# Split matmuls in attention and scan, and other rounds for front's halves, norms and weight sums: a change to a four-layer float32 kernel

## The chip, the cores and the metric

The kernel runs on one core of a Trainium2 chip. The metric is the device time of one execution in microseconds (us), as the median of several runs. A profile of one more execution shows each engine's instructions: PE (matrix products, with the weight loads as a row of their own), DVE (vector work), ACT (activation functions and copies), POOL (elementwise work beside DVE) and SP, which here only issues DMAs.

## The reference

The input x is 2 sequences of 2048 rows of 256 numbers, all float32. Four layers are added to it in turn, each on a layernorm of x:

```python
x = x + attn_a(layernorm(x))   # rmsnorm, q/kv/a = xn @ w_qkva; a linear scan along the rows, s = sigmoid(a)*s + kv; q*s
x = x + ffn(layernorm(x))      # gelu(x @ tern(W1).T + b1) @ tern(W2).T + b2, 256 -> 1024 -> 256
x = x + attn_b(layernorm(x))   # 16 heads of 64: per row, with states carried on,
                               #   G += k (k C)^T;  S += k k^T;  C += q v^T;  o = q (S C - G);  then o @ W_o
x = x + ffn(layernorm(x))      # the same weights again
```

`tern` rounds a weight matrix to -1, 0 and 1 by its own mean size.

## The kernel before

x stays on the chip as 32 chunks of 128 rows. The order of work on PE, DVE, ACT and POOL is written out by hand: each of these engines runs its instructions in the order in which the program issues them. PSUM has eight banks, which are dealt out in rings.

**Front** (`front`) does the scan layer and the first ffn. A block is four chunks (512 rows), and there are eight blocks, 0 to 7. After a start in which the first scans run, a loop makes one round per block: `ffn_in` gives eight tiles of the hidden layer (PE, then Gelu on ACT), `Hidden.split` cuts each pair of them into a rounded high half `hh` (ACT) and a rest `hl` (DVE), and `ffn_out` multiplies both by the second weight (64 matmuls) and adds the result to x. Both are generators, and `run(steps, n)` issues n pieces of one, so that other work stands between them. In rounds 0 to 3 the scan of a later block (`scan_steps`) is issued between pieces of `ffn_in`. Helpers prepare the rows of later blocks: `fs_` makes the layernorm statistics (DVE and POOL), `fq_` the normed rows (ACT), turned by a transposition in 32 x 32 squares on DVE and a way out to DRAM and back, and `fe_` the high and low halves of the turned rows (a cast on ACT, a subtraction on DVE) that `ffn_in` reads. `then` is a list of three steps that start attention's first chunk pair: its statistics, its rows, its turned rows. `later` holds the sums of attention's weights, `weights_kv`, four operations of 128 x 512 on POOL for each of wk, wv and wq.

**Attention** (`attention`) works through 32 steps: chunk n of sequence 0, then of sequence 1, for n = 0 to 15. Two steps of the same n are a pair. The products that make k, q and v of a pair (`Seven`) use a scheme with seven half-size products instead of eight, numbered 1 to 7, so they need sums of the weights (`weights_kv`) and of the turned rows (`pair_sums`, POOL). A kN or vN product is one matmul call with 512 columns, a qT product four calls with 128. One float32 matmul call is two matmul instructions, each with its weight load. The scan over rows is done in halves of 64 rows with 64 x 64 matmuls on quarters of PE's array, in bursts of 128 matmuls: `update` (hS, hM), `inter` with `products` (huT or hoT with hp), and `intra`. Between the bursts stand the products of `Seven` and the output products `outward` (hy).

**The last ffn** begins inside the last attention steps. The object `last` (class `Last`) prepares statistics, rows and halves there, and brings the rounded ffn weights back from DRAM: `weights` opens a generator of four DMAs of 256 KB, issued from ACT, and `part(n)` issues n of them; `part(None)` issues all that are left. Then a loop makes the remaining rounds. The very last block multiplies chunks 0 to 2 first and chunk 3 behind them; its result tile shares a bank with that of chunk 2.

Of the kernel before, what the change touches and what calls it, by code (L numbers as in the profile page):

```python
# [20 lines left out]
ALU = mybir.AluOpType  # L21
AX = mybir.AxisListType

P = 128
B, T, D = 2, 2048, 256
ND = D // P
# [18 lines left out]
def kernel(  # L45
# [333 lines left out]
        nc.vector.tensor_tensor(y, sc, pq, ALU.mult)  # L379
        return y  # L380

    def scan_steps(pool, g0, xnT, last, ys):

        def product(part, e):
            pq = bank([P, BT], f"pq{g0}_{e}_{part}")
            col = part * D + e * P
            for d in range(ND):
                nc.tensor.matmul(  # L388
                    pq, lhsT=wqkva[:, d, col : col + P], rhs=xnT[:, d, :], start=(d == 0), stop=(d == ND - 1),
                )  # L390
            return pq

        gate = [scan_gate(pool, g0, e) for e in range(ND)]
        for e in range(ND):
            nc.scalar.activation(gate[e], product(2, e), AF.Sigmoid)
        yield
        for e in range(ND):
            a, kq = gate[e], scan_pair(pool, g0, e)
            kv = product(1, e)
            sc = scan_line(pool, g0, e, BT, a, kq, kv, last)  # L400
            yield
            q = product(0, e)
            ys.append(kq[:, 1, :])
            nc.vector.tensor_tensor(kq[:, 1, :], sc, q, ALU.mult)
            yield
# [114 lines left out]
    def ffn_out(g0, hid, store=False, tag="ps"):  # L520

        banks = [bank([P, 2, D], f"o{g0}_{i}", tag) for i in range(2)]
        if store and g0 == blocks[-1]:
            order = [(f, range(BC - 1)) for f in range(NF)] + [(f, range(BC - 1, BC)) for f in range(NF)]
        else:
            order = [(f, range(BC)) for f in range(NF)]
        for f, cs in order:
            for c in cs:
                to = banks[c // 2][:, c % 2, :]
                for k, h in enumerate((hid.hi, hid.lo)):  # L530
                    nc.tensor.matmul(  # L531
                        to, lhsT=h[f // 2][:, f % 2, c * P : (c + 1) * P], rhs=w2r[:, f, :],
                        start=(f == 0 and k == 0 and c % 2 == 0), stop=(f == NF - 1 and k == 1),
                        skip_group_check=True,
                    )
                m = 1 if len(cs) < BC and c > 1 else 2
                if f == NF - 1 and (c % 2 == 1 or m == 1):
                    g = g0 + c + 1 - m
                    xs = x_sb[:, g : g + m, :]
                    nc.vector.tensor_tensor(xs, xs, banks[c // 2][:, c % 2 + 1 - m : c % 2 + 1, :], ALU.add)  # L540
                    if store:
                        nc.sync.dma_start(out=rows(of, g, m), in_=xs)
            yield
# [6 lines left out]
    def run(steps, n=None):  # L550
        for _ in steps if n is None else zip(range(n), steps):
            pass
# [4 lines left out]
    def front(scan_pool, ffn_pool, tern_pool, then, later):  # L557
# [21 lines left out]
        def fs_(i, between=None):  # L579
            fst[i] = norm_stats(ffn_pool, chunks(blocks[i]), bias=True, between=between)  # L580
# [89 lines left out]
        for i in range(NB):  # L670
            u, g0 = i + 5, blocks[i]
            more, scans = i + 1 < NB, u < len(units)
            hid, staged = hidden(ffn_pool, g0)
            steps = ffn_in(g0, fn.pop(i), hid, staged)
            if i == 0:
                ffn_bias(g0)
            if scans:
                ys[u] = []
                products = scan_steps(scan_pool, units[u][0], xnT[u], last[units[u][0] // CPB], ys[u])
                for j in range(4):  # L680
                    run(products, 1)
                    run(steps, 1)
                    if i == 0 and j == 0:
                        a_(4)
                        fq_(1)
                run(products)
                if i == 3:
                    fq_(5, scan_pool, "xn")
            else:
                run(steps, 4)  # L690
                if i == 4:
                    fs_(7)
                if i == NB - 2:
                    then[0]()
            if u + 1 < len(units):
                s_(u + 1)
            if i == 0:
                fs_(2)
            run(steps)
            if u + 1 < len(units):  # L700
                r_(u + 1)
            if i == 5:
                wq = const.tile([P, ND, H * DK], FP, tag="wq", name="wq")
                nc.sync.dma_start(out=wq, in_=w_q.rearrange("(c p) e -> p c e", p=P))
            if not more:
                wo = const.tile([P, NPR, D], FP, tag="wo", name="wo")
                nc.sync.dma_start(out=wo, in_=w_o.rearrange("(c p) e -> p c e", p=P))
                then[2]()

            steps = ffn_out(g0, hid, tag="out")  # L710
            if i > 3 and i - 4 < len(later):
                later[i - 4]()
            if i == 2:
                ffn_weights_away()
            if scans:
                fe_(i + 1)
                run(steps, 2)
                a_(u)
                run(steps, 3)
                if u + 1 < len(units):  # L720
                    t_(u + 1)
            if i < 3:
                fq_(i + 2)
                fs_(i + 3)
                if i == 2:
                    fs_(6)
            elif i == 3:
                fq_(6)
                fe_(5)
            elif i + 2 < NB:  # L730
                fe_(i + 2)
                if i + 3 < NB:
                    fq_(i + 3)
            if i == NB - 2:
                then[1]()
            run(steps)
            if more:
                ffn_bias(blocks[i + 1])

# [6 lines left out]
    def attention(keep, pool, state, last):  # L748
# [11 lines left out]
        def pair_sums(n):  # L760

            x = pairs[n]
            S = pool.tile([P, 4, P], FP, tag="S", bufs=1, name=f"S{n}")
            l, r = slice(0, P), slice(P, 2 * P)
            x11, x12, x21, x22 = x[:, 0, l], x[:, 1, l], x[:, 0, r], x[:, 1, r]
            for o, a, b_, op in (
                (S[:, 0, :], x21, x22, ALU.add), (S[:, 1, :], S[:, 0, :], x11, ALU.subtract),
                (S[:, 2, :], x11, x21, ALU.subtract), (S[:, 3, :], x12, S[:, 1, :], ALU.subtract),
            ):
                nc.gpsimd.tensor_tensor(o, a, b_, op)  # L770
            pairs[n] = x, S

        class Seven:

# [29 lines left out]
            def product(self, at, i, tag=None):  # L804

                new = tag is not None
                shape = [P, NPR // 2, P] if self.nm == "qT" else [P, HK]
                if new:
                    setattr(self, at, bank(shape, f"h{self.nm}{self.n}_{at}", tag))
                to = getattr(self, at)  # L810
                if self.nm == "qT":
                    for j in range(NPR // 2):
                        nc.tensor.matmul(  # L813
                            to[:, j, :], lhsT=self.B[i][:, j * P : (j + 1) * P], rhs=self.A[i],
                            start=(new and j == 0), stop=True, skip_group_check=True,
                        )
                else:
                    nc.tensor.matmul(  # L818
                        to, lhsT=self.A[i], rhs=self.B[i], start=new, stop=True, skip_group_check=True
                    )  # L820

            def add(self, c, at):
                nc.vector.tensor_tensor(self.C[c], self.C[c], getattr(self, at), ALU.add)  # L823
# [167 lines left out]

        NS = len(steps)
        pair_sums(0)
        stats = norm_stats(norm_pool, pair(1), bias=True)
        k, q, v = Seven(0, "kN", "oT"), Seven(0, "qT", "uT"), Seven(0, "vN", "oT")
        k.go(2, 1, 0, 5)
# [21 lines left out]
        for s in range(NS):  # L1018
# [24 lines left out]
                k.go(2)  # L1043
            if first and s > 0:
                units_end(s - 1)
            if s < NS - 1:
                last.part()
            if s >= 3:
                outward(s - 3, 1)
            intra(s, "S", "kN", "p1", "uT")  # L1050
# [119 lines left out]
            if s == NS - 3:  # L1170
                last.part(None)
                last.weights(False)
            if s >= 2:
                outward(s - 2, 0)
        last.out()
# [39 lines left out]
    class Last:  # L1215
# [10 lines left out]

        def stats(self, g0=None):
            g0 = self.g0 if g0 is None else g0
            self.st = [norm_stats(norm_pool, chunks(g0 + c, 2), bias=True) for c in (0, 2)]

        def rows(self, g0=None):
            g0 = self.g0 if g0 is None else g0
# [84 lines left out]
    with (  # L1317
# [7 lines left out]
        for _ in range(12):  # L1325
# [1 line left out]
        nc.scalar.activation(table, ones[:, :1], AF.Sigmoid)  # L1327
        front(
            scan_pool, ffn_pool, tern_pool, (attention_stats, attention_rows, attention_turned),
            [lambda: weights_kv(wk, wk_t), lambda: weights_kv(wv, wv_t), lambda: weights_kv(wq, wq_t)],  # L1330
        )
    front_ctx.close()

# [71 lines left out]
```

## Time and profile before

| | us |
|---|---|
| median of 3 runs | 1059.29 (1057.63 to 1059.35) |
| the profiled execution | 1060.83 |
| its span | 1059.0 |
| PE busy | 1044.0 |
| DVE busy | 730.8 |
| ACT busy | 613.4 |
| POOL busy | 201.7 |

Times inside the profile count from the start of the span. Front's rounds run from about 57 to 229 us, attention from there to about 945, the last rounds to the end. The chain that ended last lies on PE for 90% of the span. A row of a chain gives start, length, engine, tile and line; "issue" in it is time in which an engine waited for nothing that the profile shows. Ends of matmuls are modelled, so spacings from start to start are the better measure for them. A window's row gives its length, then busy time and number of instructions of PE, PE's weight loads, DVE, ACT and POOL, then the granted clock, the share of time the DMA engines were busy, and GB/s.

### The profile page before, as it was taken

The numbers are of one execution on the slowest core, as the hardware profiler recorded it, in microseconds if no ns is written. First come the engines' busy times: TensorE is split into PE (matmuls) and PEld (weight loads), VectorE is DVE, ScalarE is ACT, GpSimd is POOL, SyncE is SP. The second block draws the span as 40 slices with busy tenths as digits, with TensorE's granted clock in tenths as the row PEclk, the third lists the DMA queues.
The fourth block names the chain that finished last, engine by engine and source line by source line (L and its number), as shares of the span: only waits on it lengthen the run. The fifth ranks groups of instructions, "written<-read, shape, count | busy, mean of one in ns | idle before, by whom it ended". The sixth has DMA issues, their size and how long they took to land.

```text
span 1059.0 us, 43544 instructions
## 1 busy us (share of the span) xinstructions
PE 1044.0 (99%) x19920; PEld 805.4 (76%) x19920; DVE 730.8 (69%) x1047; ACT 613.4 (58%) x813; POOL 201.7 (19%) x314
## 2 busy tenths in 40 slices
PE   9999999999999999999999999999999999999998
PEld 7567778886777777777777777777777777889887
DVE  7987788856676765767666667666576666668873
ACT  4567778755645555455554555545545454658974
POOL 3433242831101001011010110100101020035540
PEclk9999999999999999999999999999999999999999
DMA  9231112203442423423324243243341334223321
GB/s 312 81 119 41 40 41 81 80 20 122 141 135 71 138 95 115 140 77 129 131 75 142 93 132 113 82 133 103 122 136 69 123 122 132 73 82 120 119 81 41
DMA packets 80825, 111.23 MB, mean 105 GB/s; under 512 B 8320, under 2 KB 66560, under 8 KB 80384
## 3 DMA queue, kind: packets, MB, share of 16 engines
q1 hardware_dynamic: 79024, 106.07, 30.2%
q8 instruction: 156, 2.56, 1.0%
q10 hardware_dynamic: 1584, 2.36, 0.9%
q14 instruction: 29, 0.24, 0.1%
q0 software_dynamic: 32, 0.00, 0.0%
HBM read 57.81 MB, written 50.59 MB: 102 GB/s over the span
## 4 chain that ended last, share of the span: by engine, by line
PE 90%; DVE 3%; ACT 2%; issue 2%; DMA 2%; POOL 1%; SPq 0%; ACTq 0%; DVEq 0%
PE hy L952 11%; PE o L531 9%; PE h L509 8%; PE hkN_X L818 6%; PE hqT_X L813 6%; PE hp L872 6%; PE hvN_X L818 6%; PE pq L368 4%; PE pq L388 3%; PE hS L929 3%; PE huT L889 3%; PE hoT L889 3%; PE huT L903 3%; PE hM L929 3%; PE hoT L903 3%; PE hqT_Z L813 3%
## 5 line engine op out<-in xcount | busy, mean ns | idle before, releaser
L878 DVE TENSOR_TENSOR p<-hp,mask 128x512 f32<-128x512 f32 x128 | 82.3, 683 | 83.4 <-PE hp L872 83.4
L952 PE MATMUL hy<-wo,oT 128*128 128x256 f32 x512 | 124.2, 386 | 0.0
L770 POOL TENSOR_TENSOR S<-xnT 128x128 f32<-128x128 f32 x30 | 13.8, 460 | 516.1 <-ACT xnT L312 516.1
L952 PEld LDWEIGHTS hy<-wo,oT 128*128 128x128 f32 x512 | 93.5, 190 | 20.6 <-issue 8.5
L494 DVE TENSOR_TENSOR hl<-h,hh 128x1024 fp32r<-128x1024 f32 x60 | 84.6, 1420 | 29.5 <-ACT hh L488 29.3
L515 ACT ACTIVATE h<-h,b_sb 128x512 f32<-128x512 f32 x120 | 77.9, 683 | 38.6 <-PE h L509 36.1
L914 ACT COPY uT<-huT 128x512 f32<-128x512 f32 x32 | 18.7, 586 | 124.9 <-PE huT L903 124.9
L194 ACT ACTIVATE xn<-x_sb,nb,rs 128x256 f32<-128x256 f32 x124 | 65.7, 594 | 21.9 <-POOL nb L180 20.1
L941 DVE TENSOR_TENSOR S<-S,hS 128x512 f32<-128x512 f32 x60 | 41.2, 687 | 43.2 <-PE hS L929 40.2
L259 DVE STREAM_TRANSPOSE squN<-uT 128x1024 f32<-128x1024 f32 x31 | 63.6, 2053 | 5.4 <-ACT uT L916 4.9
L971 ACT COPY uN<-rawuN 128x1024 f32<-128x1024 f32 x31 | 64.5, 2082 | 4.5 <-DMA rawuN<-dsquN 4.1
L259 DVE STREAM_TRANSPOSE sqkT<-kN 128x1024 f32<-128x1024 f32 x32 | 65.9, 2059 | 1.3 <-ACT kN L849 1.2
L971 ACT COPY kT<-rawkT 128x1024 f32<-128x1024 f32 x32 | 66.7, 2084 | 0.0
L488 ACT CAST hh<-h 128x1024 fp32r<-128x1024 f32 x60 | 63.1, 1051 | 1.9
L531 PE MATMUL o<-w2r,hl 128*128 128x256 f32 x256 | 61.3, 282 | 1.5 <-DVE hl L494 1.3
L531 PE MATMUL o<-w2r,hh 128*128 128x256 f32 x256 | 61.3, 281 | 0.0
L531 PE MATMUL o<-w2r_back,hh 128*128 128x256 f32 x248 | 60.4, 284 | 0.9 <-DVE x_sb L540 0.9
L531 PE MATMUL o<-w2r_back,hl 128*128 128x256 f32 x248 | 60.0, 281 | 0.0
L849 ACT COPY vN<-hvN_X 128x512 f32<-128x512 f32 x16 | 9.4, 587 | 78.8 <-PE hvN_X L818 78.8
L162 DVE BATCH_NORM_STATS2 st<-x_sb 128x6 f32<-128x256 f32 x128 | 51.2, 401 | 2.4 <-DMA x_sb<-in_x_dram 2.3
L823 DVE TENSOR_TENSOR kN<-kN,hkN_Y 128x512 f32<-128x512 f32 x16 | 11.0, 687 | 57.2 <-ACT kN L832 57.2
L531 PEld LDWEIGHTS o<-w2r,hl 128*128 128x128 f32 x256 | 48.2, 188 | 2.9 <-DVE hl L494 2.4
(227 smaller groups left out, 2554.3 us busy)
## 6 DMA issues: line engine op xcount, KB each, us to landing
dsqkT<-sqkT SPq DMA_DIRECT2D x32, 512.0 KB, 3.3
rawkT<-dsqkT SPq DMA_DIRECT2D x128, 128.0 KB, 3.0
dsquN<-squN SPq DMA_DIRECT2D x31, 512.0 KB, 3.3
rawuN<-dsquN SPq DMA_DIRECT2D x124, 128.0 KB, 3.1
dsqxn<-sqxn SPq DMA_DIRECT2D x14, 512.0 KB, 2.7
rawxn<-dsqxn SPq DMA_DIRECT2D x56, 128.0 KB, 2.9
out_dram<-x_sb SPq DMA_DIRECT2D x15, 256.0 KB, 2.9
x_sb<-in_x_dram SPq DMA_DIRECT2D x7, 512.0 KB, 8.9
```

The source lines that it names most:

```text
L194: nc.scalar.activation(xn[:, c, :], x_sb[:, g, :], AF.Identity, bias=nb[:, c : c + 1], scale=rs[:, c : c + 1],)
L259: nc.vector.transpose(to, src)
L494: nc.vector.tensor_tensor(self.lo[a], h, self.hi[a], ALU.subtract)
L509: nc.tensor.matmul(ph, lhsT=w1r[:, d, f * P : (f + 1) * P], rhs=r[:, d, :], start=(d == 0 and k == 0), stop=(d == ND - 1 and k == 1),)
L515: nc.scalar.activation(h[:, f % 2, :], ph, AF.Gelu, bias=b1_sb[:, f : f + 1])
L531: nc.tensor.matmul(to, lhsT=h[f // 2][:, f % 2, c * P : (c + 1) * P], rhs=w2r[:, f, :], start=(f == 0 and k == 0 and c % 2 == 0), stop=(f ...
L813: nc.tensor.matmul(to[:, j, :], lhsT=self.B[i][:, j * P : (j + 1) * P], rhs=self.A[i], start=(new and j == 0), stop=True, skip_group_check ...
L818: nc.tensor.matmul(to, lhsT=self.A[i], rhs=self.B[i], start=new, stop=True, skip_group_check=True)
L872: nc.tensor.matmul(banks[h][halves[c], p, :], lhsT=d[s][left][halves[h], p, halves[c]], rhs=d[s]["qT"][halves[h], p, halves[c]], start=Tru ...
L878: nc.vector.tensor_tensor(d[s][nm][:, h], banks[h], mask8, ALU.mult)
L952: nc.tensor.matmul(py, lhsT=d[s]["oT"][:, p, :], rhs=wo[:, p, :], start=(p == 0), stop=(p == NPR - 1),)
L971: act(t, d[s]["r" + nm].rearrange("p t q -> p q t"))
```

## The change

Five parts. Matmul calls of 512 columns are split into two of 256 columns: in `scan_steps` for rounds 2 and 3, and in `Seven` for the kN products 1, 5, 3 and the vN products 1, 5 of every pair, and also the kN products 2, 4, 6, 7 of pair 0. `Last.stats` takes four chunks in one call instead of two and two. The second returning weight is issued in one burst at the end of step `NS - 3` instead of one DMA at a time. In front, `fs_(7)`, `fe_(5)`, `fq_(7)`, `fe_(7)` and the first steps of attention move to later rounds; the weight sums of wk and wq move to the end of round 6, and those of wv behind attention's first `pair_sums`. The last block's chunk 3 gets a bank of its own.

```diff
-    def scan_steps(pool, g0, xnT, last, ys):
+    def scan_steps(pool, g0, xnT, last, ys, m=1):
...
             for d in range(ND):
-                nc.tensor.matmul(
-                    pq, lhsT=wqkva[:, d, col : col + P], rhs=xnT[:, d, :], start=(d == 0), stop=(d == ND - 1),
-                )
+                for j in range(m):
+                    r = slice(j * BT // m, (j + 1) * BT // m)
+                    nc.tensor.matmul(
+                        pq[:, r], lhsT=wqkva[:, d, col : col + P], rhs=xnT[:, d, r],
+                        start=(d == 0 and j == 0), stop=(d == ND - 1), skip_group_check=True,
+                    )
...
# ffn_out
             order = [(f, range(BC - 1)) for f in range(NF)] + [(f, range(BC - 1, BC)) for f in range(NF)]
+            banks.append(bank([P, 2, D], f"o{g0}_2"))
...
-                to = banks[c // 2][:, c % 2, :]
+                at = c // 2 if len(cs) > 1 else 2
+                to = banks[at][:, c % 2, :]
...
# front's rounds
-                products = scan_steps(scan_pool, units[u][0], xnT[u], last[units[u][0] // CPB], ys[u])
+                products = scan_steps(scan_pool, units[u][0], xnT[u], last[units[u][0] // CPB], ys[u], 2 if i > 1 else 1)
...
             else:
+                if i == 5:
+                    fs_(7)
+                elif not more:
+                    run(steps, 2)
+                    then[1]()
                 run(steps, 4)
-                if i == 4:
-                    fs_(7)
-                if i == NB - 2:
-                    then[0]()
...
             steps = ffn_out(g0, hid, tag="out")
-            if i > 3 and i - 4 < len(later):
-                later[i - 4]()
             if i == 2:
                 ffn_weights_away()
+            if i == 4:
+                fe_(5)
...
             elif i == 3:
                 fq_(6)
-                fe_(5)
-            elif i + 2 < NB:
-                fe_(i + 2)
-                if i + 3 < NB:
-                    fq_(i + 3)
-            if i == NB - 2:
-                then[1]()
+            elif i == 4:
+                fe_(6)
+            elif i == 5:
+                fq_(7)
+            elif i == 6:
+                fe_(7)
+                then[0]()
             run(steps)
             if more:
                 ffn_bias(blocks[i + 1])
+            if i == 6:
+                later()
...
# attention
+        in_two = {"kN": (1, 5, 3), "vN": (1, 5)}
+        first_in_two = {"kN": (2, 4, 6, 7), "vN": ()}
...
-                    nc.tensor.matmul(
-                        to, lhsT=self.A[i], rhs=self.B[i], start=new, stop=True, skip_group_check=True
-                    )
+                    m = 2 if i in in_two[self.nm] or self.n == 0 and i in first_in_two[self.nm] else 1
+                    for j in range(m):
+                        cols = slice(j * HK // m, (j + 1) * HK // m)
+                        nc.tensor.matmul(
+                            to[:, cols], lhsT=self.A[i], rhs=self.B[i][:, cols],
+                            start=(new and j == 0), stop=True, skip_group_check=True,
+                        )
...
         pair_sums(0)
+        weights_kv(wv, wv_t)
         stats = norm_stats(norm_pool, pair(1), bias=True)
...
-            if s < NS - 1:
+            if s < NS - 2:
                 last.part()
+            elif s == NS - 2:
+                last.part(None)
...
                 last.weights(False)
+                last.part(4)
...
# Last.stats
-            self.st = [norm_stats(norm_pool, chunks(g0 + c, 2), bias=True) for c in (0, 2)]
+            st = norm_stats(norm_pool, chunks(g0), bias=True)
+            self.st = [[t[:, c : c + 2] for t in st] for c in (0, 2)]
...
-            [lambda: weights_kv(wk, wk_t), lambda: weights_kv(wv, wv_t), lambda: weights_kv(wq, wq_t)],
+            lambda: (weights_kv(wk, wk_t), weights_kv(wq, wq_t)),
```

## The prediction

> **What bounds the kernel now.** I read the page's first part and its queues, then the waits, then windows one pair of attention steps long, then the chain at each place where PE had to wait.
>
> ```profile
> PE 1044.0 (99%) x19920; PEld 805.4 (76%) x19920; DVE 730.8 (69%) x1047; ACT 613.4 (58%) x813; POOL 201.7 (19%) x314
> ...
> q8 instruction: 156, 2.56, 1.0%
> ```
>
> PE is the bound; another engine counts only where PE stands still for it. The second line is PE's own code arriving: 156 packets of 2.56 MB / 156 = 16.4 KB. PE ran 19920 matmuls, 19920 weight loads and 116 semaphore and drain instructions, 39956 / 156 = 256 a packet. So the code comes in blocks of 256.
>
> Windows of one pair of steps (us, then busy time and count of PE, weight loads, DVE, ACT, POOL):
>
> ```profile
> 442.90:486.00 43.10, 43.10 (x1144) 32.63 (x1143) 28.56 (x39) 22.13 (x28) 3.11 (x8) 1.00 0.35 113
> 486.00:529.10 43.10, 43.10 (x1141) 32.63 (x1140) 28.59 (x39) 22.19 (x28) 3.11 (x8) 1.00 0.35 118
> 529.10:572.50 43.40, 43.40 (x1141) 32.84 (x1140) 28.55 (x39) 22.12 (x28) 3.11 (x8) 1.00 0.31 100
> ...
> 745.40:790.10 44.70, 43.46 (x1141) 32.78 (x1140) 28.62 (x39) 22.23 (x28) 3.10 (x8) 1.00 0.34 112
> 790.10:834.50 44.40, 43.35 (x1144) 32.66 (x1143) 28.53 (x39) 22.24 (x28) 3.12 (x8) 1.00 0.33 109
> 834.50:880.20 45.70, 43.52 (x1141) 32.81 (x1140) 28.78 (x42) 23.18 (x30) 6.82 (x13) 1.00 0.39 119
> ```
>
> The same work takes 43.1 or up to 45.7 us at a full clock (1.00). The chain says where it goes:
>
> ```profile
> 776.05 0.93 PE hp L872 x63
> 776.98 1.24 issue
> 778.22 0.21 PE hp L872
> ```
>
> PE stops inside a burst of small matmuls and waits for nothing the profile shows. Numbering PE's instructions in the trace, the pauses at 291, 777, 826, 868, 873 and 914 us all fall on instruction 192 or 193 modulo 256; call 192 place 0. Before each, a code packet had just come: it landed at 776.85 and PE went on at 778.22, 1.4 us later. From entering one block to being able to enter the next took 3.5 us (289.15 to 292.67; 823.69 to 827.14), and 4.8 to 5.4 us in the pair at 834. A burst of 128 small matmuls is 256 instructions, a whole block, in 2.0 us. It outruns the fetch when it begins at a block's edge; if it begins mid-block, the large matmuls between bursts stretch most blocks to 4.2 us and the shortest to 3.4.
>
> Two other stalls:
>
> ```profile
> 164.66 3.05 DMA rawxn<-dsqxn
> 167.73 2.31 ACT xhl L202
> ...
> 172.26 1.29 DVE x_sb L540 x2
> 173.55 2.27 DVE hl L494 x2
> ...
> 1052.57 1.03 DVE x_sb L540 x2
> 1053.64 2.19 PE o L531 x16
> ```
>
> In front's round 4, ACT waits for `fe_(5)`'s rows, so the Gelus, `hl` and then PE come late: the second products take 9.37 us, against 7.47 in rounds 6 and 7. At the end PE waits until DVE has read the bank that chunk 3 shares with chunk 2.
>
> **The padding.** A middle pair is 1140 matmuls + 1140 loads + 4 semaphore instructions = 2284, or 9 x 256 - 20, so its bursts slide by 20 places a pair. The change splits five kN and vN products; each is two instructions of 512 columns, so 10 matmuls and 10 loads are added: 2304 = 9 x 256, and the place stays. It stays where the sum puts it: +96 in front (12 `product` tiles x 2 d x 2 instructions, each one matmul and load more), +36 in pair 0 (9 products x 4), +20 for each of pairs 1 and 2. The first burst of the pair at 313.5 moves from place 67 to 67 + 172 = 239.
>
> Pair lengths of before by that burst's place: 67, 47, 27, 7, 243: 43.1 to 43.2 us; 223: 43.4; 203, 183, 163, 143: 43.2, 43.4, 43.2, 43.1; 123: 44.7; 103: 44.4; 83: 45.7. Place 239 lies between 0 and 0.3 us late; I take 0.1. The 13 pairs from 313.5 to 880.2 us take 566.7, and 13 x 43.1 = 560.3: 6.4 us late now, 13 x 0.1 = 1.3 then, gain 5.1. Pair 0 loses the 1.4 us pause at 291 (the burst goes from place 0 to 160); 0.3 may return, gain 1.1. In the last pair the pause at 914 (about 0.6) goes, but bursts then start at places 3 to 46; gain 0.2. Together 6.4 us, bounds 2 (a 3.4 us block now lies in every pair, and a late packet may hit each) and 8.4 (no pause left).
>
> The splitting costs 216 more matmuls. A 512-column one starts 430 ns after the last and a 256-column one 216, so 2 ns each, 0.4 us; the second load (190 ns) hides under 216.
>
> [...]
>
> **The last bank.** The wait from 1052.42 to 1053.64 is 1.2 us against a spacing of 0.12: 1.1 us go. DVE has 2.27 us free after it, so the end moves too. I take 1.0 (0.8 to 1.1).
>
> **Front.** Gone: round 4's 1.9 us (`fe_(5)` leaves the end of round 3, where ACT stood on its DMA) and round 5's 8.35 - 7.47 = 0.9, where the wv sums on POOL stretched `hl` from 1.23 to 2.1-3.3 us. New: `fe_(5)` and `fe_(7)` run one round before use. ACT ends its hidden casts 10.6 us into a round (208.23 + 1.05 - 198.71); cast 2.1 and subtraction 2.2 more give 14.9, and PE needs it at 7.46 + 7.47 = 14.9: a tie, for which I put 0.3 us in all (0 to 1.5).
>
> The sums of wk and wq now follow round 6's statistics and `ffn_bias(7)` on POOL:
>
> ```profile
> 191.20 2.27 POOL L466 TENSOR_TENSOR wv_t<-wv 128x512 f32<-128x512 f32 x1
> ...
> 210.88 1.30 POOL L466 TENSOR_TENSOR wq_t<-wq 128x512 f32<-128x512 f32 x1
> ...
> 228.90 0.46 POOL L770 TENSOR_TENSOR S<-xnT_first 128x128 f32<-128x128 f32 x1 [10.50 <-PE o L531]
> ```
>
> Eight operations take 10.3 us at 1.29, or 18 at 2.27 beside a busy DVE; I take 13. They start some 5.4 us into round 7 (the statistics leave DVE at 1.2, as they follow `fe_(7)`; then 1.6 us of POOL and 2.6 of `ffn_bias`) and end at 18.4, and `pair_sums(0)` waits behind them, needed by the fifth product of k at 15.0 + 1.7 = 16.7 plus 0.46 for itself. PE stalls about 2 us (0 to 4). Then four sums of wv stand ahead of the statistics of pair 1, whose norm rows on ACT stand ahead of the copy of kN that frees v's bank: 0.5 us (0 to 2). Front's sum: -2.8 + 0.3 + 2.0 + 0.5 = 0 (-2.8 to +4).
>
> **The rest.** Four-chunk statistics issue four POOL operations for eight (0.22 + 0.71 + 0.19 + 0.22 us a set); POOL had idled 29 us before, rows come at most 0.6 us later and their halves are due a round on: 0, and 0.6 without that cover. The second weight burst issues four 256 KB DMAs from ACT near 891 us; three more issues at 0.33 hold uN's copy (891.67) by 1.0, and its use is the update at 900.8: 0. The three issues removed from the next step were hidden. [...]
>
> **Sum.** -6.4 + 0.4 - 1.0 + 0 = -7.0. The profiled execution took 1060.83 us (span 1059.0), 1.54 over the median 1059.29; taking the same 7.0 off both: 1053.8 profiled, 1052.3 as median.
>
> **Rivals.** (a) Fixed at a bad place: if PE's instructions before attention are not as I count, every pair keeps the wrong place. The three bad rows cost (1.6 + 1.3 + 2.6) / 3 = 1.8; 13 x 1.8 - 6.4 = +17, so 1076. It decides from 116 instructions down (place 123) or 100 up (83); a few semaphore waits more don't reach that. Chance 0.04. (b) POOL becomes the bound where attention starts: stalls of 4 + 2 with a gain of 3 in the fetch: -3 + 0.4 - 1.0 - 2.8 + 6.3 = 0, so 1059. It decides if the eight sums take 18 us; for it speaks 2.27, against it 1.30. Chance 0.07. (c) The padding does nothing, because pauses follow DMA traffic and not the place: -1.0 + 0.4 + 0 gives 1058.7; against it, clean pairs have the same traffic (DMA share 0.35 and 0.34). Chance 0.07. The forecast: 0.82.
>
> **How the numbers follow.** Best ends: -8.4 + 0.4 - 1.1 - 2.8 = -11.9; worst: -2 + 0.4 - 0.8 + 4 + 1.5 = +3.1. The ends seldom meet: 1048.0 to 1058.5 leaves out about one in ten on each side. This kernel can be told from no change at about 0.2%, 2.1 us. Faster by more: the forecast with little of (b), 0.83. Within: (c) and part of (b), 0.10. Slower: (a) and the worst of front, 0.07.
>
> **What would show it.** Windows of every middle pair at 43.1 to 43.3 us and no "issue" piece over 0.5 us in them; round 4's second products at 7.5 us; no wait for DVE x_sb at the end; POOL's S some microseconds after the first products of k. Pairs at 44 or more throughout, or pauses away from block edges, would make it wrong.

## The result, and the profile after

The changed kernel takes 1060.91 us (median of 22 runs, 1057.79 to 1063.34) against 1057.89 us for the kernel before on the same chip (22 runs): ratio 1.0025, 95% interval 1.0016 to 1.0033. It is slower by a quarter of a per cent, where the prediction had it faster by 0.7%. Its profiled execution took 1063.03 us with a span of 1061.1, 2.2 and 2.1 more than that of before. Both profiled executions lie above their kernel's median.

The page's first part and its queue of code:

```profile
PE 1047.8 (99%) x20136; PEld 848.9 (80%) x20136; DVE 729.7 (69%) x1047; ACT 612.6 (58%) x813; POOL 181.8 (17%) x282
...
q8 instruction: 157, 2.57, 1.0%
```

216 matmuls more, as counted, and one code packet more. Where the time went is read by laying the two traces over each other: the start of each matmul of after minus the start of the same matmul of before, here called the lag. It goes to -2.3 us by 194 us (rounds 4 and 5), is -1.85 at 228, then jumps to +4.2 at the start of attention, falls to -0.2 by 874 through the pairs, and rises to +1.3 through the last pair and to +3.3 by 1028; the last bank takes 1.2 back, which leaves +2.1. Three places lose time, then: attention's start, the last pair, the last rounds.

**Attention's start.** The waits of PE, after (engine, tile and line, what it waited for: us in total, times, longest):

```profile
PE hkN_Z L832 <- POOL S L778: 2.8, 1, 2.8
PE hoT L918 <- issue: 1.9, 2, 1.7
PE o L536 <- DVE hl L497: 1.1, 3, 0.4
...
PE huT L918 <- issue: 0.5, 1, 0.5
```

The first did not exist before. The chain there, with POOL's sums in front of `S`:

```profile
223.75 2.23 POOL wk_t L472
225.98 1.25 POOL wq_t L469
...
229.75 1.27 POOL wq_t L472
231.01 0.42 POOL S L778
231.43 0.04 issue
231.47 2.08 PE hkN_Z L832 x4
```

and the windows that follow (the granted clock is the number behind POOL's column):

```profile
224.00:228.00 4.00, 4.00 (x29) 3.66 (x28) 2.12 (x3) 1.13 (x1) 3.92 (x3) 1.00 0.00 1
228.00:232.00 4.00, 1.17 (x5) 0.72 (x4) 0.69 (x1) 0.58 (x1) 3.92 (x6) 0.85 0.00 0
232.00:236.00 4.00, 4.00 (x15) 3.49 (x14) 0.00 (x0) 0.59 (x1) 3.92 (x5) 0.50 0.02 4
236.00:240.00 4.00, 4.00 (x21) 3.62 (x20) 0.76 (x2) 1.17 (x2) 3.15 (x6) 0.80 0.00 0
```

PE is busy for all of 232 to 236 us but does 15 matmuls where 29 went into the window at 224: at 231.47 its sums are there, but its clock is granted at 0.50. The clock's record has 0.5 from 230.80 to 237.63 us, 6.83 us. The lag splits the loss: -1.85 to +1.16 over the wait (3.0), +1.16 to +4.24 over the slow clock (3.1).

The second of these is the price of this execution. The mean granted clock of the 22 runs was 0.996 in four of them (the profiled one is among these), 0.997 in three, 0.998 in eleven and 0.999 or 1.0 in four, so the slow stretch is not the same every time. Two kernels below that have the same wait were profiled with a slow stretch of 3.41 us (mean clock 0.998); it cost 1.8 us in both.

**The middle pairs.** Windows of five of the 13 middle pairs, after:

```profile
446.04:489.55 43.51, 43.41 (x1152) 34.73 (x1151) 28.52 (x39) 22.14 (x28) 3.10 (x8) 1.00 0.34 113
532.76:575.90 43.14, 43.14 (x1151) 34.55 (x1150) 28.53 (x39) 22.16 (x28) 3.11 (x8) 1.00 0.36 116
575.90:619.46 43.56, 43.40 (x1151) 34.73 (x1150) 28.54 (x39) 22.16 (x28) 3.11 (x8) 1.00 0.35 114
792.84:835.98 43.14, 43.14 (x1151) 34.55 (x1150) 28.59 (x39) 22.14 (x28) 3.12 (x8) 1.00 0.35 113
835.98:880.00 44.02, 43.48 (x1152) 34.74 (x1151) 28.57 (x42) 23.22 (x30) 5.83 (x9) 1.00 0.41 126
```

The place is the same in all 13 pairs, 242 (239 was forecast), and none takes 44.4 or 45.7 us any more, as three did before. But 43.56 is not 43.14: six of the first 12 pairs are up to 0.42 us late, each by a stop at place 0 inside a burst of small matmuls.

**The last pair** has the one long stop that is left, in the chain:

```profile
897.78 0.74 PE hoT L918 x49
898.52 1.69 issue
900.21 0.46 PE hoT L918 x15
```

It is at place 0. PE had entered the block at 894.00, and the packet of the next block did not start until 897.57. Over the pairs before (320 to 850 us) a packet starts 0.76 us after its block was entered (median). Under way then were the four DMAs of `w2r`, issued from 890.66 to 893.7 and landed from 894.1 to 900.8.

**The end** runs through without the wait for `x_sb` that before had:

```profile
1045.98 4.21 PE h L512 x18
1050.19 7.73 PE o L536 x64
```

### The profile page after: what moved, and what is told of

It reads as the page before. It is cut to its first block, busy times and chain, and to the rows that moved or that the text cites. A ratio compares the mean times of both kernels' runs of the same rounds, so it can differ in the third digit from the quotient of the medians.

```text
span 1061.1 us, 43929 instructions
## 1 busy us (share of the span) xinstructions
PE 1047.8 (99%) x20136; PEld 848.9 (80%) x20136; DVE 729.7 (69%) x1047; ACT 612.6 (58%) x813; POOL 181.8 (17%) x282
## 4 chain that ended last, share of the span: by engine, by line
PE 84%; DVE 5%; ACT 3%; issue 3%; POOL 2%; DMA 2%; SPq 1%; ACTq 0%; POOLq 0%; DVEq 0%
PE hy L967 10%; PE hkN_X L832 6%; PE hp L887 6%; PE hqT_X L824 6%; PE hvN_X L832 6%; PE o L536 5%; PE h L512 5%; PE pq L368 4%; PE pq L390 4%; PE huT L904 3%; PE hoT L904 3%; PE huT L918 3%; PE hS L944 3%; PE hoT L918 3%; PE hkN_Z L832 3%; PE hM L944 3%
```

## The experiments

Each kernel is timed beside the kernel before on its chip; ratios are to that. "Early sums" stands for the kernel of the third experiment, on which most of the later ones build.

### The splits alone

The kernel before with `scan_steps` and `Seven` split as in the change, nothing else.

> The kernel before with the split matmuls alone. Theory (pauses at code-block edges set by the place of the bursts): the 1.4 us pause of pair 0 goes, the middle pairs keep one place near 240 and lose at most 0.4 us each instead of up to 2.6; by the trace of after that is -1.1 in pair 0 and -3.1 in the middle pairs, so about 4 us less than before (2.5 to 6). Rival (what was gained in the pairs of after came from its later start and other DMA traffic, not from the place): within 1 us of before, with pauses at other places.

Measured: 1057.81, ratio 0.9982 (0.9965 to 0.9999); the profiled execution took 1057.67, 3.2 less than that of before. By the ratio that is 1.9 us, less than the 2.5 to 6 expected. Place 239 in all pairs, as the sum of the prediction had it. The first 12 pairs took 519.33 us, against 520.98 before and 12 x 43.14 = 517.7: 0.14 late a pair. The lag was -6.4 at 874 us, what the prediction had for the whole of attention, and the last rounds gave 2.9 of it back. So the splits do what they were forecast to do up to the last pair, and the kernel behind them keeps half.

One reading of before falls here: this kernel's front is that of before but for the split products of rounds 2 and 3, and `fe_(5)` stands where it stood, yet it ran 1.4 us ahead by 181 us. The transfer `dsqxn`, issued at 159.2 us, took 2.62 us here and 3.93 in before, and ACT's wait for `rawxn` was 1.39 us instead of 2.83. So most of the 1.9 us of round 4, which the prediction took off for `fe_(5)`, goes without moving it. Whether that transfer differs from execution to execution or by the splits is not shown.

### Front's moves alone

The kernel before with front's other rounds for norms and halves, and the weight sums moved:

```diff
-            if i > 3 and i - 4 < len(later):
-                later[i - 4]()
...
+            if i == 6:
+                later()   # wk, wq; wv behind attention's first pair_sums
```

> The kernel before with front's moves and the weight sums' new place alone. Theory (PE waits 2.8 us for POOL's sums where attention starts, and its clock is then granted at a half for some 7 us): -2.4 in rounds 4 and 5, +6.3 at the start of attention, so +3.9 (3 to 5), and a granted clock of 0.5 near 231 to 238 us. Rival (the dip of the clock is an accident of one execution): 2.8 - 2.4 = +0.4 and no dip.

Measured: 1064.54, ratio 1.0033 (1.0011 to 1.0056). The wait for `S` is there with the same length, and the clock after it is at half for 3.41 us:

```profile
228.00:232.00 4.00, 1.18 (x3) 0.30 (x2) 0.69 (x2) 0.58 (x1) 3.92 (x5) 1.00 0.00 0
232.00:236.00 4.00, 4.00 (x12) 2.57 (x11) 0.00 (x0) 0.58 (x1) 3.92 (x6) 0.57 0.00 0
```

The lag is -1.7 before the wait, +1.3 behind it and +3.1 at 236 us: this part alone makes the kernel slower, by about as much as the whole change did (the two intervals overlap).

### The sums early

```diff
             if i == 4:
+                weights_kv(wk, wk_t)
                 fe_(5)
-            if i == 6:
-                later()
+            if i == 6:
+                weights_kv(wq, wq_t)   # ahead of the round's ffn_out; wv as in the change
```

> After, with the sums of wk back in round 4 and those of wq at the start of round 6's second products; wv's stay in attention. Theory: PE finds pair_sums in time, no wait for POOL, clock 1.0 throughout, so 5.5 to 6.3 us less than after, about 3 below before. Rival (POOL beside DVE in round 4 stretches hl and gives the same back in front): less than 3 us below after, with PE waiting for hl in rounds 4 and 6.

Measured: 1056.51, ratio 0.9966 (0.9950 to 0.9982), faster than before. The same stretch of the windows:

```profile
228.00:232.00 4.00, 4.00 (x27) 3.72 (x26) 0.69 (x1) 1.73 (x3) 3.92 (x6) 1.00 0.01 4
232.00:236.00 4.00, 4.00 (x28) 3.64 (x27) 2.69 (x3) 1.35 (x4) 3.40 (x6) 1.00 0.00 0
```

28 matmuls in the window that had 15, at a full clock. POOL does the same sums, only earlier, and the end moves from +2.1 to -4.4 of lag. This one order of POOL's work is worth 6.5 us and decides the sign of the change.

### PE kept busy through the wait

```diff
-        k.go(2, 1, 0, 5)
+        k.go(2, 1, 0)
+        idle = bank([P, P], "idle")
+        for _ in range(12):
+            nc.tensor.matmul(idle, lhsT=ident, rhs=ident, start=True, stop=True)
+        k.go(5)
```

> After, with 12 unused 128 x 128 matmuls (2.7 us) in the place where PE waits for POOL's sum. Theory (the second half of the loss is the clock, which falls because PE stands still): the wait is filled, the clock stays at 1.0, and 3.0 to 3.5 us of after's time go though PE does more work. Rival (the slow matmuls behind the wait have another cause, such as POOL's traffic): the same time as after, with the spacing of the 128-column matmuls still doubled.

Measured: 1059.28, ratio 0.9982 (0.9965 to 0.9999). The products whose operand POOL still owes come no sooner (lag +1.2 at the end of the wait, as in the change), but the clock stays whole and the lag is +1.3 at 240 us where the change had +4.3, which shows that the second half of the loss is the clock's and not POOL's. The kernel then meets a pause of 2.07 us in the last pair and pays there (the last of these windows is at 0.60):

```profile
230.00:234.00 4.00, 3.82 (x27) 3.47 (x27) 0.04 (x1) 0.58 (x1) 3.92 (x6) 1.00 0.01 4
234.00:238.00 4.00, 4.00 (x29) 3.74 (x28) 1.70 (x2) 1.22 (x3) 3.84 (x5) 1.00 0.00 0
...
892.00:896.00 4.00, 1.93 (x93) 1.75 (x86) 2.54 (x4) 1.74 (x3) 1.71 (x4) 0.97 0.56 168
896.00:900.00 4.00, 4.00 (x63) 2.81 (x65) 0.29 (x1) 1.38 (x2) 0.00 (x0) 0.60 0.43 153
```

The fillers also moved the bursts by 48 instructions, to place 34, and there the 12 pairs took 517.70 us: 43.14 each, none late.

### Two other places

Early sums, and `product` split in more rounds: one more round gives place 34, two more give place 82.

```diff
-                ... ys[u], 2 if i > 1 else 1)
+                ... ys[u], 2)                  # place 82
+                ... ys[u], 2 if i > 0 else 1)  # place 34
```

> The kernel with the early sums (sums of wk in round 4, of wq in round 6) and one thing more: front's `product` matmuls are split in all eight rounds, 48 matmuls more, 96 instructions of PE, which do the same work. Every burst of attention moves from place 242 to place 82; the traffic stays. Theory 1 (the place of the bursts sets the pauses): in before the pair whose first burst lay at place 83 took 45.7 us and that at 103 took 44.4, so the 13 middle pairs take 44.4 to 45.7 us each, against 43.14 to 43.5 with the early sums alone; 15 to 25 us more, about 1076. Rival (pauses follow the DMA traffic, whatever the place): pairs as with the early sums alone, time within 1 us of theirs plus 0.1 us for the splits.

> The kernel with the early sums and `product` split in rounds 1 to 7 instead of 2 to 7: 24 matmuls, 48 instructions of PE more. Bursts move from place 242 to 34. Theory 1 (place): the small pauses of 0.2 to 0.4 us at a block's edge inside a burst go, since no block's edge then falls late in a burst; all 12 whole pairs take 43.14 us as in the kernel with the filler, which had this place: 517.7 in all against 519.3, so 1.6 us faster than the early sums alone in the pairs, about 1055; in the last pair bursts lie elsewhere too, which may give or take 1. Rival (traffic): no change. A second rival: round 1 with split matmuls is short of code, since it follows the loads: 1 to 2 us lost before 100 us.

Measured at place 82: 1063.7, ratio 1.0055 (1.0038 to 1.0072); at 34: 1055.08, ratio 0.9970 (0.9957 to 0.9982). Pairs at 82, then at 34:

```profile
486.11:529.73 43.62, 43.41 (x1151) 34.63 (x1150) 28.53 (x39) 22.21 (x28) 3.10 (x8) 1.00 0.35 112
529.73:573.44 43.71, 43.41 (x1151) 34.64 (x1151) 28.52 (x39) 22.21 (x28) 3.11 (x8) 1.00 0.34 112
```

```profile
483.03:526.16 43.13, 43.13 (x1151) 34.56 (x1150) 28.57 (x39) 22.14 (x28) 3.10 (x8) 1.00 0.33 109
785.00:828.14 43.14, 43.14 (x1152) 34.56 (x1151) 28.50 (x39) 22.13 (x28) 3.12 (x8) 1.00 0.35 118
```

The DMA share is the same (0.33 to 0.35), the place is not, and the pairs follow the place: 12 pairs take 521.96 us at 82, 517.67 at 34, 519.2 to 520.3 at 242 (six kernels). So the rival that pauses follow traffic is out for the middle pairs. But the price of place 82 is (521.96 - 517.67) / 12 = 0.36 us a pair, not the 1.3 to 2.6 that the expectation and the prediction's rival (a) took from three rows of before. The rest of the loss at 82 lies elsewhere: the pause near 291 us is back (1.4), the pair at 835 us takes 45.27 instead of 43.44 (1.8). That last pair explains one of the three rows: before's 45.7 us at place 83 was this same pair, in which weights of the last ffn come back beside the common work, so its price does not hold for the others. The rows of places 103 and 123 had no padded kernel to test them. In the kernel with front's moves alone, whose bursts slide as in before, a pair at place 106 took 44.70 us and one at 126 took 43.11, so the place of the first burst alone does not fix an unpadded pair's time; why is open. At place 34 nothing is lost before 100 us (lag -0.06, against -0.08 with the early sums), so the second rival falls. The gain of the pairs (1.6 us) was mostly lost again in the last pair, behind a pause of 2.38 us and another dip of the clock.

### The burst of weights

```diff
-            if s < NS - 2:
-                last.part()
-            elif s == NS - 2:
-                last.part(None)
+            if s < NS - 1:
+                last.part()
...
                 last.weights(False)
-                last.part(4)
```

First on the early sums, then at place 34 as well, then at place 34 with `last.part(2)` in place of `last.part(4)`, which was meant as half a burst.

> The kernel with the early sums, with the last layer's weights issued as in before (one part in every step up to the last but one, and no burst in the last step). Theory (the burst of 1 MB on ACT's queue holds up PE's code packet in the last pair): the pause of 1.9 us near 890 us goes, and the lag behind before falls by 1.5 to 2 us there; the end comes 1.5 to 2 us sooner, about 1054.7. Rival (the pause is the place of the last pair's bursts, at a block's edge whatever is loaded): the pause stays, time within 0.5 us of the early sums. Second rival: the part issued in the step before lengthens that step's fetches, as in before's pair at 834 us (45.7): 1 us lost there.

> The early sums, `product` split in rounds 1 to 7 (place 34), and the last layer's weights issued one part a step as in before (no burst). Theory (place 34 clears the whole pairs, and in the last pair the burst of 1 MB is what makes the pause of 2.4 us and the dip of the clock behind it): whole pairs at 43.14 us; no pause over 1.2 us in the last pair; end 1 to 2 us sooner than with place 34 and the burst, 1053 to 1054.5 as median, span about 1052.5. Rival (the last pair's packets come late with any loading, and the loss only spreads over more block edges, as the kernel with the early sums and no burst suggested, whose three pauses of 0.5 to 1.0 us took back what the one had cost): no change within 0.5 us of place 34 with the burst.

> The same, but the burst is halved: two parts of w2r (512 KB) at once in the last pair, the other two in the step after. Theory (the code packet waits behind the burst's bytes, so its delay goes with them): the pause at the block's edge near 892 us falls from 2.4 us to 0.8 to 1.4, with no dip of the clock; the end 0.8 to 1.5 us sooner than with the whole burst. Rival (any transfer under way at a block's edge delays its packet as much): pause of 2 us or more stays, no gain.

Measured: without the burst on the early sums 1055.2, ratio 0.9969 (0.9956 to 0.9981), no gain that can be told; its trace ends 0.4 us later. At place 34 without the burst 1054.2, ratio 0.9953 (0.9936 to 0.9970); with `last.part(2)` 1056.15, ratio 0.9975 (0.9964 to 0.9986), on the same chip. The last pair with the burst (place 34), then without:

```profile
888.00:892.00 4.00, 1.79 (x91) 1.47 (x90) 2.46 (x8) 1.74 (x3) 1.71 (x4) 1.00 0.45 172
892.00:896.00 4.00, 3.83 (x46) 3.13 (x46) 1.28 (x1) 0.69 (x1) 0.00 (x0) 0.58 0.74 252
```

```profile
888.00:892.00 4.00, 4.00 (x137) 3.38 (x136) 2.46 (x8) 2.40 (x4) 1.72 (x4) 1.00 0.51 135
892.00:896.00 4.00, 3.87 (x118) 3.04 (x120) 3.78 (x5) 3.42 (x6) 0.00 (x0) 1.00 0.39 110
```

The stop of 2.38 us and the half clock behind it are gone, and the trace ends 1.5 us sooner. The packets go with it: from entering a block near the burst to the start of the next block's packet it took 2.9 to 4.5 us in every one of the nine kernels that have the burst, where 0.76 us is the median in the pairs. Without the burst packets also start late now and then (up to 2.6 us after 880 us at place 34); that they meet the single parts of 256 KB is the author's reading. The kernel before had one of 3.9 us at 882 us, which PE did not feel, since its block lasted 6.2.

`last.part(2)` did not halve the burst. The next step, which issues what is left, follows so soon that all four DMAs go out within 1.4 us, as they do within 1.3 us with `last.part(4)` at the same place (start, length, and the issues on ACT's queue):

```profile
883.83 0.33 ACTq L459 DMA_DIRECT2D w2r_back<-dw2r  x1
884.20 0.45 ACTq L459 DMA_DIRECT2D w2r_back<-dw2r  x1
884.86 0.81 ACTq L459 DMA_DIRECT2D w2r_back<-dw2r  x2
```

So what half a burst costs was not tested. This is a second kernel with the burst at place 34 (a packet 3.67 us late, a stop of 1.50), timed on the same chip as the one without: its runs took 1055.45 to 1056.93 us, those without the burst 1053.23 to 1055.46.

On the early sums at place 242 the last pair came out 0.8 us better without the burst, but the pair before it took 44.25 us instead of 43.44, as the second rival had it, and the other 12 took 0.4 more. So the burst's cost is shown at place 34 (1.5 us in both traces, 2.0 by the medians of one chip); at place 242 spreading it gained nothing.

### The bank of the last chunk

The early sums, with chunk 3's sums in the bank of chunk 2 as in before.

> The kernel with the early sums, with the last chunk's sums in the bank that it shares with the chunk before it, as in before. Theory (PE waits there until DVE has added chunk 2): a wait of PE for x_sb of 0.9 us returns and the end comes 0.8 to 1.1 us later. Rival (the end hangs on DVE's last additions, not on PE): no change.

Measured: 1057.64, ratio 0.9985 (0.9969 to 1.0001). The wait is back:

```profile
PE o L534 <- DVE x_sb L543: 0.9, 1, 0.9
```

With a bank of its own the lag falls by 1.2 at that place in after and with the early sums alike; here it stays as it was (+0.08 ahead of it, +0.05 behind). The step is worth 1.2, a little more than the 0.9 of the wait, as the prediction's spacing from start to start had it. The rest of this trace's difference to the early sums lies in the 13 middle pairs (1.3) and the last pair (1.8, a pause of 2.51 us with a half clock behind it).

### The statistics of four chunks

`Last.stats` undone to two sets of two chunks, on the early sums and then on the change itself.

> The kernel with the early sums, with the statistics in two sets of two chunks as in before. Theory 1 (the four-chunk statistics make the rows of the norms late, so the halves in the last layer's rounds and PE's waits for `hl` between 970 and 1020 us come from them): those waits, 0.8 us in the kernel with the early sums, fall to 0 to 0.2, and the end comes about 0.7 to 1.2 us sooner. [...]

> The changed kernel with one thing undone: the statistics in two sets of two chunks, as in before. Theory (the eight POOL operations of two sets, for four, run beside DVE's `hl` and slow it; the four-chunk sets earned about 2 us with the early sums): PE's waits for `hl` in the last rounds grow from 0.7 us to 2 or more, and the kernel is 1 to 2 us slower than the change, some 1061 to 1063. Rival (in the change PE comes to the last rounds later, as late as in before, and waits for no `hl` there in either form, as before had none): within 0.5 us of the change.

Measured: on the early sums 1056.77, ratio 0.9990 (0.9979 to 1.0001); on the change 1061.54, ratio 1.0023 (1.0009 to 1.0037), which is the change's own ratio. PE's waits for `hl` from 925 us on, first in the early sums with two sets, then in the change with two sets:

```profile
PE o L536 <- DVE hl L497: 2.6, 6, 0.8
```

```profile
PE o L536 <- DVE hl L497: 1.4, 4, 0.4
```

With four chunks in a set both have 2 waits, of 0.8 and 0.7 us. POOL's four operations of a set, in the last rounds of the early sums with two sets and then with one (the last figures are the busy time and the mean of one in ns; the fourth operation of a set has 3.9 and 4.1 us):

```profile
L175 POOL TENSOR_TENSOR rs<-rs,mhalf 128x2 f32<-128x2 f32 x10 | 7.1, 714 | 0.8
L179 POOL TENSOR_TENSOR nb<-mv,rs 128x2 f32<-128x2 f32 x10 | 6.6, 664 | 0.8
L180 POOL TENSOR_SCALAR nb<-nb 128x2 f32<-128x2 f32 x10 | 6.0, 602 | 0.9
```

```profile
L175 POOL TENSOR_TENSOR rs<-rs,mhalf 128x4 f32<-128x4 f32 x5 | 6.2, 1232 | 0.4
L179 POOL TENSOR_TENSOR nb<-mv,rs 128x4 f32<-128x4 f32 x5 | 1.4, 276 | 0.4
L180 POOL TENSOR_SCALAR nb<-nb 128x4 f32<-128x4 f32 x5 | 1.2, 233 | 0.4
```

23.6 us of POOL against 12.9. It is not the size alone: in before the same 128x2 operations took 0.71, 0.19 and 0.22 us near 252 us. So the four-chunk sets cost nothing, against the first expectation: the waits grew without them. On the early sums they save 2.3 us of trace; in the change the last rounds lose 2.0 us with them and 2.9 without, and the times tell no difference, so the second expectation (1 to 2 us slower) is not borne out either.

## Why the prediction was wrong

By its own steps, in us of the profiled execution:

| step | forecast | by the lag |
|---|---|---|
| front's rounds 4 and 5 | -2.5 | -1.85 |
| PE waits for `S` behind POOL's sums | +2.0 | +3.0 |
| the clock after that wait | not in the sum | +3.1 |
| wv's sums ahead of pair 1's statistics | +0.5 | 0 |
| pair 0 | -1.1 | -1.4 |
| 13 middle pairs, with the splits' own cost | -4.7 | -3.1 |
| last pair, with the burst | -0.2 | +1.5 |
| last rounds | 0 | +2.0 |
| last bank | -1.0 | -1.2 |
| sum | -7.0 | +2.1 |

**The step that failed is "PE stalls about 2 us (0 to 4)".** It named the wait, the engine, the operation and the queue in front of it, and the length was within its bounds: eight sums took 14.1 us for the 13 taken (those of wk 2.2 to 2.3 each, those of wq 1.28). What failed is its price: it took the wait by its length alone, and this wait cost its length (3.0) and the slow clock behind it (3.1). Rival (b) had this mechanism and no term for the clock either; it came to 1059. With 3.0 + 3.1 for 2.0 + 0.5 alone, the sum would have been -3.4 and the forecast 1055.9. So this step explains 3.6 of the 9.1 us between forecast and trace, more than any other, and without it the change is faster than before (the early sums, 0.9966); the rest is spread over the last rounds (2.0), the last pair (1.7), the middle pairs (1.6) and smaller terms. The prediction's own worst ends added up to +3.1, which covers the trace; its range stopped at 1058.5 because the ends seldom meet. They did not meet here either: of the largest losses, the slow clock stood in no term of the sum and the last rounds stood in it at 0.

**The last pair was mis-sized.** The sum had 0 for what the burst does to PE's code, and its worst end had 1.5, an estimate of the author's; no run shows that term. What the runs showed in its place: beside the burst a code packet started 2.9 to 4.5 us after its block was entered, in nine kernels of nine, against a median of 0.76 us in the pairs. The row came out 1.7 above its forecast in the change. Without the burst it is +0.1 with the splits alone and +0.8 with the early sums; with it, but two sets of statistics, it is +0.5. So the burst's share of the 1.7 is argued, not shown.

**The padding was right in kind.** The sum of instructions held (239 alone; 242 with all of the change), the pairs of 44.4 to 45.7 us are gone, and pair 0's pause is gone. The size of a pair's lateness was taken as 0.1 from a range of 0 to 0.3; over the 13 pairs it is (563.64 - 13 x 43.14) / 13 = 0.22, and 0.15 in the 12 pairs without the last as a mean of six kernels at 242. Rival (a) took 1.8 a pair; at place 82, the one place of its rows that was tested, it is 0.36. Rival (c) falls.

**Front's gain was taken from one execution.** 1.9 us for `fe_(5)` was mostly one DMA's late landing (3.93 us in before, 2.62 with the splits alone): with the splits alone and `fe_(5)` in its old place, 1.4 of it were gone as well.

**The last rounds** were taken to keep what came before them. The change loses 2.0 there and the splits alone 2.9; all 12 kernels with the splits lose 1.3 to 4.6, while front's moves alone lose nothing. In the change most of it sits at four matmuls that read `hl`, and 0.7 of it are waits that the profile counts. Why `hl` comes late to PE only with the splits is open.

**The clock.** Six waits of PE of 2.07 to 2.84 us were each followed by a stretch at half clock, 3.41 us long five times and 6.83 once; waits of 1.69 to 1.97 us were not. The clock's record shows more. Its stretches within the work are whole numbers of 3.413 us long (in the change 225.28 us is 66 of them, 6.83 is 2 and 822.61 is 241), so the record can be cut into such steps. In the six waits 2.07 to 2.82 us lay within one step, and the clock halved where that step ended; of the others at most 1.72 us lay in one step. The mean clock of the six executions was 0.998 five times and 0.996 once (the change), that of the other profiled ones 1.0. How much of a wait falls into one step depends on when it comes. That would fit the differing clocks of the 22 runs, but no execution of the change with a whole clock was profiled.

## What to carry to other kernels

A wait of PE is not priced by its length alone: here the clock halved behind every wait of 2.07 us or more and behind none of 1.69 to 1.97, so look at the granted clock in the windows behind a wait, and add the slow stretch (3.41 or 6.83 us here) to the price; if the wait can't be removed, try filling it with work (12 unused matmuls kept the clock at 1.00 here). Before sums are moved to another engine's quiet place (POOL's eight took 14.1 us), ask what that engine must deliver first when the next stage begins, and put that ahead in its queue or the sums a round earlier. PE's code came in packets of 256 instructions here, and 12 pairs took 517.67 us at place 34 and 521.96 at 82: count instructions to see where bursts of short ones fall in a block, and test whether large DMA bursts can be kept away from the edges (at place 34 the trace without the burst ended 1.5 us sooner). Before a DMA burst is called halved, read in the trace when its parts were issued.

The version that all this points to has the lowest ratio here, though its interval overlaps with that of the early sums: the change with the sums early, `product` split in rounds 1 to 7, and without the burst, 1054.2 us against 1058.78 for before, ratio 0.9953 (0.9936 to 0.9970).

## What the runs showed of the hardware

- The clock of PE halved after waits of 2.07, 2.38, 2.51, 2.82, 2.83 and 2.84 us, for 3.41 us five times and 6.83 us once; after 1.69, 1.84, 1.87 and 1.97 us it did not. Each slow stretch began at the end of a 3.413 us step of the clock's record in which PE had stood still for 2.07 us or more.
- A code packet starts 0.76 us (median) after PE has entered the block before it. Beside 1 MB of DMAs issued on ACT's queue within 1.3 to 3.0 us one started 2.9 to 4.5 us after, in nine kernels of nine. Such a burst is not the only way to a late packet: at place 82, 11 of the 13 middle pairs had one of 3.3 to 5.2 us.
- With bursts at place 34 the 12 pairs ahead of the weights' return took 43.14 us in four kernels (one pair 43.22), with the same DMA share as elsewhere: no stop at a block's edge was left in them.
